# A graph network on one core: some columns of source rows selected by TensorE instead of gathered

## The chip, the cores and the metric

The kernel runs on one core of a Trainium2 chip. The metric is the device time of one execution in microseconds; the figure for the kernel before is the median of 3 runs, 18,531.41 us (18,529.7 to 18,533.06). The core has TensorE (PE, matrix products), VectorE (DVE), ScalarE (ACT), GpSimd (POOL) and SyncE (SP). The first four have instruction queues of their own and meet through semaphores; POOL issues the indirect DMAs (gathers and scatters) and SP the plain ones.

## What is computed

A graph has 12,500 nodes with 32 features and 400,000 edges `src -> dst`, sorted by `dst`. Three attention layers and one edge network run over it:

```
def _gat(x, edge_index, W, att_s, att_d, bias, heads, ch, neg_slope):
    h = (x @ W.T).reshape(n, heads, ch)
    a_s = (h * att_s[None]).sum(-1)
    a_d = (h * att_d[None]).sum(-1)
    src, dst = (edge_index[0], edge_index[1])
    logits = jax.nn.leaky_relu(a_s[src] + a_d[dst], neg_slope)
    m = jax.ops.segment_max(logits, dst, num_segments=n)
    ex = jnp.exp(logits - m[dst])
    denom = jax.ops.segment_sum(ex, dst, num_segments=n)
    alpha = ex / (denom[dst] + 1e-16)
    out = jax.ops.segment_sum(alpha[:, :, None] * h[src], dst, num_segments=n)
    return out.reshape(n, heads * ch) + bias
...
e_feat = jnp.concatenate([x[rol], x[col], edge_attr], axis=-1)
h = jax.nn.relu(e_feat @ W1 + b1)
v = h @ W2 + b2
x_cand = jax.ops.segment_max(v, col, num_segments=num_nodes)
return jnp.maximum(x_cand, x[:, -v.shape[-1]:])
...
x = _layernorm(x + _L0_gnn_ref(x, ...))
x = _layernorm(x + _L1_gnn_ref(x, edge_index, edge_attr_32, ...))
```

Layers 1 and 2 have two heads of 16 channels, with an elu and a clip between the layers; layer 3 has one head of 32. What matters here is `h[src]` and `a_s[src]`, and `x[rol]` in the edge network: for every edge a row of a node table is needed, in an order that only the data know.

## The kernel before

The edges lie on 128 partitions, 3,125 consecutive edges on each; "column t" is edge t of every partition. The work goes through the columns in chunks of T = 60, with four shorter chunks at the end (48, 32, 29 and 16), 54 chunks per stage. There are four stages: `attention(1)`, `attention(2)`, `attention(3)` and `edge_network`; stage 2 and the edge network go through the columns backwards.

For each chunk, `gather` (line 68) issues one indirect DMA per column. It fetches 128 rows, one for each partition, from a table in DRAM (`table1`, or `tables[2]` to `tables[4]`) into a tile `g` (`xs` in the edge network), by the row numbers in `src_i`, `src_last` or `src_first`. So each stage has 3,125 gathers, all in POOL's queue. `gpool` has four `g` buffers and POOL runs ahead of the others by as many chunks as there are free buffers. A row of table 1 holds 36 numbers, those of the later tables 34, 33 and 32.

The rest of a chunk in an attention stage is a chain over DVE, ACT and PE. DVE forms the logits (`lg`, line 697), a running maximum by a scan (line 704), ACT their exponentials (line 715), DVE multiplies the gathered rows with them (`gf`, line 723) and sums them along each run of equal `dst` by scans (line 734). `divided` (lines 494 to 501) divides by the sum and adds the bias. In stages 1 and 2 `finish` then forms the elu on ACT (lines 510 to 512, 521) and goes through the chunk in four blocks of 16 columns (12 in the last): `yb` (line 523), a transpose to `yt` (line 525), two matmuls with the next layer's weights (lines 528 and 529), transposes back to `tb` and `at` (lines 531 and 532). In stage 3 `finish3` adds the node's own row and runs a layer norm on DVE and ACT. Sums go to `sums`, the rows of the next table to `tables[li + 1]`, both by SP's DMAs. In the edge network a chunk has, for each of four blocks, three transposes (lines 870 to 872), twelve half-passes of matmuls (line 877), two activations, two more products (line 883) and a transpose back (line 884), then scans, a maximum, an addition and a layer norm.

Since a node's row is written once per edge of the run, the later tables are indexed by edge: `last_i` and `first_i` hold, for each of the 98 x 128 nodes, the row where its run ends or begins. Between stages a few small transfers join the runs that cross a partition's edge (`s`, `merge_i`), and 98 scatters (`move`, lines 624 to 627) put the input rows where stage 3 reads them. At the start there are 98 gathers of `found` and 98 scatters of `give`; at the end 98 gathers of `so` bring the result into node order.

The order of the instructions on each engine is set when the kernel is built: a scheduler lays out the whole program, by dependences and by its own estimate of when things come due. Each engine then runs its own list in that order.

Of the kernel before, what the change touches and what calls it, by code (L numbers as in the profile page):

```python
# [24 lines left out]
def gnn_resnorm_kernel(ctx: ExitStack, tc: tile.TileContext, a: dict, out: bass.AP):  # L25

# [13 lines left out]
    nc = tc.nc  # L40
# [42 lines left out]

    groups = [(c0, min(28, NC - c0)) for c0 in range(0, NC, 28)]
# [19 lines left out]
    gpool = gstack.enter_context(tc.tile_pool(name="g", bufs=4, side="right"))  # L104
# [4 lines left out]
    x0 = runs.tile([P, NC, D], F32, name="x0")  # L109
# [22 lines left out]
    fixed = ctx.enter_context(tc.tile_pool(name="fixed", bufs=1, space=PSUM)).tile([P, 512], F32, name="fixed")  # L132
    own = const.tile([P, 1], F32, name="own")
    nc.gpsimd.iota(own, pattern=[[1, 1]], base=E + NN, channel_multiplier=1,
                   allow_small_or_imprecise_dtypes=True)
    zeros = const.tile([P, 1250], F32, name="zeros")
# [59 lines left out]

    table1 = dram.tile([NN, D + 4], F32, name="table1")
# [10 lines left out]
    def clear(table, part=0, parts=1):  # L208
        flat = edge_rows(table).rearrange("p t w -> p (t w)")
        k = TE * table.shape[1] // parts  # L210
        z = next(z for z in range(1250, 0, -1) if k % z == 0)
# [86 lines left out]
    cont = runs2.tile([P, TE + 1], F32, name="cont")  # L298
    src_last = runs2.tile([P, TE], I32, name="src_last")
# [14 lines left out]
    with tc.tile_pool(name="seg", bufs=1) as sp, tc.tile_pool(name="rowsp", bufs=2) as rp, \  # L314
# [52 lines left out]
        for c0, n in groups:  # L367
            rows = rp.tile([P, 28, SB], I32, name="found")
            for c in range(n):
                gather(rows[:, c, :], dst_d, find_i[:, c0 + c:c0 + c + 1])  # L370
            less = rp.tile([P, 28, SB], BF16, name="less")[:, :n, :]
            nc.vector.tensor_tensor(less, rows[:, :n, :], bcast(node_p[:, c0:c0 + n, None], [P, n, SB]), op=ALU.is_lt)
            nc.vector.tensor_reduce(r[:, c0:c0 + n], less, axis=AX.X, op=ALU.add)
            nc.vector.tensor_add(first[:, c0:c0 + n], first[:, c0:c0 + n], r[:, c0:c0 + n])
# [15 lines left out]
        nc.sync.dma_start(out=node_rows(table1), in_=tb)  # L390

# [111 lines left out]
    def finish(li, pool, psum, den, v, n, hb=1):  # L503

        y = pool.tile([P, D * T], F32, name="y")[:, :D * n].rearrange("p (f t) -> p f t", t=n)
# [11 lines left out]
        for b in range(0, n, TB):  # L517
# [8 lines left out]
            ph = psum.tile([P, TB * D], F32, name="ph", bufs=hb)[:, :w]  # L526
# [3 lines left out]
            at = pool.tile([P, TB, D], F32, name="at")[:, :nt, :]  # L530
# [19 lines left out]
    def finish3(pool, psum, den, v, x, n):  # L550
# [4 lines left out]
        layernorm(pool, den[:, 2 * T:], x, n)  # L555

    def empties():
# [4 lines left out]
        with tc.tile_pool(name="empty", bufs=2) as ep, tc.tile_pool(name="emptyps", bufs=1, space=PSUM) as eps:  # L562
# [66 lines left out]
    def attention(li, idx):  # L629
# [10 lines left out]
        with tc.tile_pool(name=f"s{li}", bufs=2) as sp, tc.tile_pool(name=f"f{li}", bufs=2) as fp:  # L640
# [18 lines left out]
            with tc.tile_pool(name=f"ps{li}", bufs=1, space=PSUM) as psp, \  # L659
                    tc.tile_pool(name=f"fps{li}", bufs=1, space=PSUM) as fps:  # L660

                small_p = psp.tile([P, 512], F32, name="small_p")
                den = small_p[:, 128:]
                old = None
                for c, (t0, n) in enumerate(todo):
                    g = gpool.tile([P, T * (D + 4)], F32, name="g")[:, :n * w].rearrange("p (t w) -> p t w", w=w)
                    for t in range(n):
                        gather(g[:, t, :], table, idx[:, t0 + t:t0 + t + 1])
# [44 lines left out]
                    rx = psp.tile([P, heads, 512], F32, name="rx", bufs=3 - heads)  # L713
# [5 lines left out]
                    for h in range(heads):  # L719
                        nc.scalar.activation(  # L720
                            rx[:, h, :FS * (n + 1)].rearrange("p (k t) -> p k t", t=n + 1),
                            bcast(rr[:, h:h + 1, :], [P, FS, n + 1]), AF.Exp)
                        nc.vector.tensor_mul(v[:, h * wd:h * wd + ch, cur].rearrange("p f t -> p t f"),  # L723
                                             g[:, :, h * ch:(h + 1) * ch], bcast(wt[:, h, :, None], [P, n, ch]))
                        nc.scalar.copy(v[:, h * wd + ch, cur], wt[:, h, :])  # L725
# [4 lines left out]
                    for h in range(heads):  # L730
                        for f in range(0, wd, FS):
# [226 lines left out]
```

## Time and profile before

| what | value |
|---|---|
| median of 3 runs | 18,531.41 us |
| the profiled execution, its own time | 16,382.21 us |
| its span, first to last instruction | 16,379.3 us |
| gathers of `g` and `xs`, lines 68 | 4 x 3,125 |
| POOL busy | 12,218.7 us (75%) |
| DVE busy | 6,836.7 us (42%) |
| ACT busy | 2,899.1 us (18%) |
| PE busy | 2,781.3 us (17%) |
| mean granted PE clock | 0.578 of full speed |

The four stages show up in a table of busy time by stretch. The columns after the stretch and its length are busy microseconds and instruction counts of PE, its weight loads (PEld), DVE, ACT and POOL, then the granted clock, the share of the DMA engines and GB/s:

```profile
350.00:4250.00 3900.00, 618.47 (x812) 214.74 (x812) 1450.33 (x2532) 799.68 (x1140) 2933.02 (x3099) 0.56 0.27 59
4450.00:8230.00 3780.00, 566.60 (x796) 206.58 (x796) 1387.15 (x2332) 774.32 (x1108) 2859.00 (x3022) 0.57 0.22 44
8450.00:12180.00 3730.00, 0.00 (x0) 0.00 (x0) 1344.37 (x1553) 487.81 (x453) 2820.63 (x2984) 0.50 0.24 54
12310.00:16180.00 3870.00, 1483.15 (x3244) 640.80 (x3244) 2347.93 (x2578) 720.17 (x873) 2910.53 (x3079) 0.68 0.24 65
```

The profile is one execution, and its own time is given beside its span; it differs from the median of the runs by 2,149 us. A line of the groups names line, engine, operation, tiles and count, then busy microseconds and the mean nanoseconds of one, then the idle time just before and what ended most of it. A timeline line has start and duration in microseconds, and in brackets the idle time before and its releaser.

### The profile page before, as it was taken

What the parts mean: (1) busy time and instruction counts of PE and PEld (TensorE: products, weight loads), DVE (VectorE), ACT (ScalarE), POOL (GpSimd) and SP (SyncE); (2) the same over time, 40 slices, a digit from 0 to 9 for tenths busy, and PEclk for the clock granted to TensorE, in tenths of its full rate; (3) what the DMA queues carried; (4) which work ended last, traced back from release to release, by engine and by line L of the source; (5) the groups of instructions that cost most, each with busy time, mean ns of one, the idle gap of its engine ahead of it and who ended that gap; (6) DMA issues with size and microseconds to landing.
All of it is one profiled execution on the core that took longest, in us unless ns stands there. A gap on an engine that the chain in (4) does not pass through costs nothing.

```text
span 16379.3 us, 42394 instructions
## 1 busy us (share of the span) xinstructions
PE 2781.3 (17%) x5140; PEld 1116.2 (7%) x5140; DVE 6836.7 (42%) x9700; ACT 2899.1 (18%) x3835; POOL 12218.7 (75%) x12921
## 2 busy tenths in 40 slices
PE   0111111111111111111100000000003333334342
PEld 0000000000000000000000000000001111111110
DVE  2433333333333333333333333333335666666654
ACT  0221212121212222121211111111111111111111
POOL 6777777777777777777777777777767777777775
PEclk5555555555555555555555555555556666666676
DMA  4222222222222222222222222222222222222221
GB/s 59 71 60 69 60 55 73 55 48 42 43 41 47 41 44 44 43 45 41 46 47 58 51 56 53 56 53 55 54 57 59 66 66 64 66 66 64 69 63 42
DMA packets 580809, 897.63 MB, mean 55 GB/s; under 512 B 286271, under 2 KB 490238, under 8 KB 567070
## 3 DMA queue, kind: packets, MB, share of 16 engines
q0 software_dynamic: 413088, 226.62, 12.5%
q1 hardware_dynamic: 167116, 665.01, 11.5%
q10 hardware_dynamic: 304, 3.20, 0.1%
q14 instruction: 259, 2.11, 0.0%
q8 instruction: 42, 0.69, 0.0%
HBM read 390.67 MB, written 503.27 MB: 55 GB/s over the span
## 4 chain that ended last, share of the span: by engine, by line
POOL 71%; issue 23%; DMA 3%; DVE 1%; PE 0%; ACT 0%; POOLq 0%; DVEq 0%; ACTq 0%
POOL g L68 52%; POOL xs L68 17%; DMA g<-table,src_i 1%; DMA g<-table,src_last 1%; DMA xs<-table,src_last 1%; DMA g<-table,src_first 1%; POOL give L72 1%; POOL so L68 1%; POOL x_e L72 1%; PE ph L877 0%; DMA s<-sums,at_i 0%; PE pv L883 0%; DVE vf L887 0%; DVE z L803 0%; ACT xd L889 0%
## 5 line engine op out<-in xcount | busy, mean ns | idle before, releaser
L68 POOL DMA_INDIRECT g<-table,src_i x3125 | 2958.5, 947 | 989.6 <-issue 940.2
L68 POOL DMA_INDIRECT g<-table,src_last x3125 | 2957.1, 946 | 952.7 <-issue 938.1
L68 POOL DMA_INDIRECT xs<-table,src_last x3125 | 2954.9, 946 | 955.4 <-issue 936.8
L68 POOL DMA_INDIRECT g<-table,src_first x3125 | 2955.7, 946 | 952.7 <-issue 940.8
L697 DVE TENSOR_TENSOR lg<-g,af 128x60 f32<-128x60 f32 (+4 forms) x270 | 59.3, 250 | 4422.3 <-DMA g<-table,src_first 2333.3
L528 PE MATMUL ph<-yt,w_bd 128*128 128x512 f32 (+2 forms) x840 | 669.2, 893 | 3434.1 <-DVE yt L525 3434.1
L529 PE MATMUL pa<-yt,a_bd 128*128 128x512 f32 (+2 forms) x840 | 656.7, 878 | 3307.4 <-DVE at L532 3307.0
L877 PE MATMUL ph<-xt,wb_bd 128*128 128x512 f32 (+2 forms) x832 | 466.1, 645 | 2419.0 <-DVE xt L870 2419.0
L683 DVE CAST src_last<-g 128x60 int32<-128x60 f32 (+4 forms) x54 | 12.7, 235 | 2056.4 <-DMA g<-table,src_i 2056.4
L738 ACT COPY rows<-mx 128x120 f32<-128x120 f32 (+3 forms) x162 | 49.9, 308 | 4419.8 <-DVE mx L704 4366.5
L737 ACT COPY rows<-gf 128x2040 f32<-128x2040 f32 (+3 forms) x162 | 628.4, 3879 | 648.4 <-DVE gf L734 648.4
L734 DVE TENSOR_TENSOR_SCAN gf<-rx,gf 128x488 f32<-128x488 f32 (+4 forms) x918 | 731.9, 858 | 1.4 <-ACT gf L725 0.9
L591 PE MATMUL pt<-ident,tops 128*34 128x128 f32 (+1 forms) x3 | 1.0, 322 | 3954.6 <-DVE xr L548 3952.9
L723 DVE TENSOR_TENSOR gf<-g,small_p 128x960 f32<-128x960 f32 (+5 forms) x270 | 597.8, 2214 | 63.1 <-ACT small_p L715 63.1
L523 DVE SCALAR_TENSOR_TENSOR yb<-y,pe 128x512 f32<-128x512 f32 (+2 forms) x420 | 268.7, 640 | 605.2 <-ACT pe L521 586.7
L533 ACT COPY tb<-at 128x32 f32<-128x32 f32 (+4 forms) x420 | 92.3, 220 | 2333.8 <-DVE at L532 2333.8
L528 PEld LDWEIGHTS ph<-yt,w_bd 128*128 128x128 f32 x840 | 218.6, 287 | 3845.7 <-DVE yt L525 3367.3
L879 ACT ACTIVATE ht<-ph,b_c 128x512 f32<-128x512 f32 (+2 forms) x416 | 275.1, 661 | 1144.0 <-PE ph L877 1140.2
L529 PEld LDWEIGHTS pa<-yt,a_bd 128*128 128x128 f32 x840 | 220.3, 278 | 3681.9 <-DVE at L532 3511.5
L877 PE MATMUL ph<-et,wb_bd 128*128 128x512 f32 (+2 forms) x832 | 450.1, 626 | 0.0
L877 PE MATMUL ph<-xst,wb_bd 128*128 128x512 f32 (+2 forms) x832 | 431.2, 602 | 34.3 <-DVE xst L872 34.3
L883 PE MATMUL pv<-ht,w_bd 128*128 128x512 f32 (+2 forms) x832 | 415.3, 593 | 6.1 <-DVE vf L884 2.0
(295 smaller groups left out, 8591.8 us busy)
## 6 DMA issues: line engine op xcount, KB each, us to landing
sums<-rows SPq DMA_DIRECT2D x100, 1080.0 KB, 4.2
table<-tb SPq DMA_DIRECT2D x50, 1020.0 KB, 4.1
sums<-rows SPq DMA_DIRECT2D x50, 1020.0 KB
g<-table,src_i POOLq DMA_INDIRECT x3125
x_e<-zeros SPq DMA_DIRECT2D x10, 5000.0 KB, 16.8
g<-table,src_last POOLq DMA_INDIRECT x3125
g<-table,src_first POOLq DMA_INDIRECT x3125
xs<-table,src_last POOLq DMA_INDIRECT x3125
```

The lines of the kernel that those rows point to most:

```text
L68: return nc.gpsimd.indirect_dma_start(out=dst, out_offset=None, in_=table, in_offset=bass.IndirectOffsetOnAxis(ap=idx, axis=0))
L72: return nc.gpsimd.indirect_dma_start(out=table, in_=src, in_offset=None, out_offset=bass.IndirectOffsetOnAxis(ap=idx, axis=0))
L523: nc.vector.scalar_tensor_tensor(yb, y[:, :, b:b + nt], 3.0, pe, op0=ALU.min, op1=ALU.add)
L528: nc.tensor.matmul(ph, lhsT=w_bd, rhs=yt, start=True, stop=True)
L529: nc.tensor.matmul(pa, lhsT=a_bd, rhs=yt, start=True, stop=True)
L533: nc.scalar.copy(tb[:, b:b + nt, D:], at[:, :, :heads])
L723: nc.vector.tensor_mul(v[:, h * wd:h * wd + ch, cur].rearrange("p f t -> p t f"), g[:, :, h * ch:(h + 1) * ch], bcast(wt[:, h, :, None], [ ...
L734: nc.vector.tensor_tensor_scan(turned(gf[:, o:o + k], rev), turned(rx[:, h, :k], rev), turned(gf[:, o:o + k], rev), 0.0, op0=ALU.mult, op1 ...
L737: nc.scalar.copy(rows[:, :, :gw], v[:, :, cur].rearrange("p f t -> p t f"))
L877: nc.tensor.matmul(ph, lhsT=wb_bd[:, s, h, :], rhs=x, start=(s == 1), stop=(s == 0))
L879: nc.scalar.activation(ht, ph, AF.Relu, bias=b1_c[:, h:h + 1])
L883: nc.tensor.matmul(pv, lhsT=w2_bd[:, h, :], rhs=hts[h], start=(h == 0), stop=(h == 1))
```

## The change

In stages 1 to 3 one column in 7 and in the edge network one in 12 is no longer gathered row by row. Instead all 12,544 node rows (98 x 128) are held in SBUF, split into three bf16 parts whose sum is the f32 row (`parts`), and TensorE selects the rows. Node number n is written as q, n's partition (n divided by 98), k, one of 7 groups of columns, and b, one of 14 columns in the group. For one column of edges, `fetch` does this:

- two matmuls (L252 of the changed kernel) spread `q + 128 k` of the 128 edges over all partitions (`places_p`);
- DVE compares it with `kid`, giving 7 one-hot matrices 128 x 128 in bf16 (`oh`, L255), and makes a mask for b (`bm`, L258);
- 21 matmuls (7 groups x 3 parts, L262) add up in PSUM (`acc`) the 14 node rows of the right partition and group;
- DVE masks all but the right one (`mine`, L265) and sums over the 14 (L266) into the column of `g`.

In stage 1 the parts come from the node table that is in SBUF anyway; before stages 2, 3 and 4 `node_parts` gathers the node rows with 98 gathers. `Fetch` works out q, k and b for all its columns at the start of a stage. To make room, `g` and `xs` have three buffers instead of four, `rows`, `y`, `at` and `ph` one instead of two, the tile of zeros is half as long, `found` comes in groups of 14, the small PSUM tiles move into `fixed`, `rx` is split by head and its scans follow each head's product, and the edge network's `z` is written over `xs`.

```
+    KT, KN = 7, 14
+    EVERY = {1: 7, 2: 7, 3: 7, 4: 12}
...
-    gpool = gstack.enter_context(tc.tile_pool(name="g", bufs=4, side="right"))
+    xpool = gstack.enter_context(tc.tile_pool(name="x", bufs=1, side="right"))
+    gpool = gstack.enter_context(tc.tile_pool(name="g", bufs=3, side="right"))
...
+    small_p, places_p = fixed[:, 128:384], fixed[:, 384:]
...
+    def split(pool, k, rows, w):
+        rows = rows.rearrange("p b w -> p w b")
+        hi, mid, lo = (parts[:, i, k, :KN * w].rearrange("p (w b) -> p w b", b=KN) for i in range(3))
+        r = pool.tile([P, D + 4, KN], F32, name="rest")[:, :w, :]
+        nc.scalar.copy(hi, rows)
+        nc.vector.tensor_sub(r, rows, hi)
+        nc.scalar.copy(mid, r)
+        nc.vector.tensor_sub(r, r, mid)
+        nc.scalar.copy(lo, r)
...
+        def __contains__(self, t):
+            return bool(self.every) and t < TE // self.every * self.every and t % self.every == self.every - 1
+
+        def fetch(self, psum, g, t, to, bufs=2):
+            if t not in self:
+                return
+            pool, w, i = self.pool, self.w, t // self.every
+            for j in range(2):
+                nc.tensor.matmul(places_p, lhsT=bcast(self.at[:, j, i:i + 1], [P, P]), rhs=ident_b,
+                                 start=(j == 0), stop=(j == 1))
+            oh = pool.tile([P, KT, P], BF16, name="oh")
+            nc.vector.tensor_tensor(oh, bcast(places_p[:, None, :], [P, KT, P]), bcast(kid[:, :, None], [P, KT, P]),
+                                    op=ALU.is_equal)
+            bm = pool.tile([P, KN], F32, name="bm")
+            nc.vector.tensor_scalar(bm, count[:, :KN], self.b[:, i:i + 1], None, op0=ALU.is_equal)
+            acc = psum.tile([P, 512], F32, name="acc", bufs=bufs)[:, :KN * w]
+            for k in range(KT):
+                for part in range(3):
+                    nc.tensor.matmul(acc, lhsT=oh[:, k, :], rhs=parts[:, part, k, :KN * w],
+                                     start=(k == part == 0), stop=(k == KT - 1 and part == 2))
+            mine = pool.tile([P, D + 4, KN], F32, name="mine")[:, :w, :]
+            nc.vector.tensor_mul(mine, acc.rearrange("p (w b) -> p w b", b=KN), bcast(bm[:, None, :], [P, w, KN]))
+            nc.vector.tensor_reduce(g[:, to, :w], mine, axis=AX.X, op=ALU.add)
+
+    def node_parts(li, idx, w):
+        with tc.tile_pool(name=f"np{li}", bufs=2) as pool:
+            for k in range(KT):
+                rows = pool.tile([P, KN, D + 2], F32, name="noderows")[:, :, :w]
+                for b in range(KN):
+                    gather(rows[:, b, :], tables[li], idx[:, k * KN + b:k * KN + b + 1])
+                split(pool, k, rows, w)
...
                     for t in range(n):
-                        gather(g[:, t, :], table, idx[:, t0 + t:t0 + t + 1])
+                        if t0 + t not in fetch:
+                            gather(g[:, t, :], table, idx[:, t0 + t:t0 + t + 1])
+                    for t in range(n):
+                        fetch.fetch(psp, g, t0 + t, t)
...
                 for t in range(n):
-                    gather(xs[:, t, :], tables[4], src_last[:, t0 + t:t0 + t + 1])
+                    if t0 + t not in fetch:
+                        gather(xs[:, t, :], tables[4], src_last[:, t0 + t:t0 + t + 1])
+                for t in range(n):
+                    fetch.fetch(pfp, xs, t0 + t, t, bufs=1)
...
-                z = vp.tile([P, T, D], F32, name="z", bufs=1)[:, :n, :]
+                z = xs[:, :n, :]
```

The scheduler's order on DVE in a chunk of stage 1, from the list of instructions of the changed kernel: after y (L585) come the first oh of the next chunk, then the four blocks of `finish`, with the first `mine` after the first transpose and the second oh in the last block; then for each further column `mine`, the next column's oh, the sum. On PE the 21 matmuls of a column stand directly ahead of the two small ones of the next column. In stage 3 all columns' passes stand behind the layer norm of the chunk before, and in stage 4 too, where the last `mine` follows `xf` and three of its scans.

## Prediction

> **What bounds the kernel now.** I read the page first: shares, then the chain that ended last, then the groups.
>
> ```profile
> PE 2781.3 (17%) x5140; PEld 1116.2 (7%) x5140; DVE 6836.7 (42%) x9700; ACT 2899.1 (18%) x3835; POOL 12218.7 (75%) x12921
> ...
> POOL 71%; issue 23%; DMA 3%; DVE 1%; PE 0%; ACT 0%; POOLq 0%; DVEq 0%; ACTq 0%
> ...
> L68 POOL DMA_INDIRECT g<-table,src_i x3125 | 2958.5, 947 | 989.6 <-issue 940.2
> ```
>
> Four groups of 3125 gathers fill the kernel: 0.947 us each and 0.30 us of issue between two, 1.25 us per gather, 75 us per chunk of 60. POOL and its issue are 94% of the chain. VectorE (DVE) works 42%, but what counts is the length of its own chain in a chunk. The timeline of DVE in stage 1:
>
> ```profile
> 1017.65 0.21 DVE L683 CAST src_last<-g 128x60 int32<-128x60 f32 x1 [39.72 <-DMA g<-table,src_i]
> ...
> 1043.30 2.15 DVE L501 TENSOR_TENSOR y<-y,fixed 128x1920 f32<-128x1920 f32 x1
> 1051.76 0.69 DVE L523 SCALAR_TENSOR_TENSOR yb<-y,pe 128x512 f32<-128x512 f32 x1 [6.30 <-ACT pe L521]
> ```
>
> DVE sat idle 39.7 us until the gathers were in. Its waits in stage 4 (12310 to 16180 us) look different:
>
> ```profile
> DVE xt L870 <- PE ph L877: 347.5, 99, 5.5
> DVE xst L872 <- DMA xs<-table,src_last: 321.6, 68, 17.7
> DVE et L871 <- PE ph L877: 275.1, 103, 5.1
> ```
>
> Columns: us in total, times, longest. Over 52 chunks DVE waits only 6.2 us per chunk for gathers; 75.05 - 6.2 = 68.9 us are its chain with TensorE and ScalarE. In stage 3 one chunk's chain runs from 10022.4 to 10053.0, 30.6 us.
>
> The speed of TensorE (PE) comes from two places of its timeline:
>
> ```profile
> 40.49 2.24 PE L335 MATMUL p_all<-under,is_hi 128*128 128x99 bf16 x25 [4.74 <-DVE under L329]
> ```
>
> ```profile
> 14060.46 2.07 PE L877 MATMUL ph<-xt,wb_bd 128*128 128x512 f32 x2 [45.71 <-DVE xt L870]
> 14062.33 1.92 PE L877 MATMUL ph<-et,wb_bd 128*128 128x512 f32 x2
> 14064.03 1.56 PE L877 MATMUL ph<-xst,wb_bd 128*128 128x512 f32 x2
> 14065.43 1.02 PE L877 MATMUL ph<-xt,wb_bd 128*128 128x512 f32 x2
> 14066.29 1.02 PE L877 MATMUL ph<-et,wb_bd 128*128 128x512 f32 x2
> ```
>
> 25 bf16 pairs of weight load and matmul take 2.24 us, 81 ns apart, so the loads hide. After 45.7 us of idleness a record of 512 columns comes every 0.85 us; 4.5 us later every 0.43.
>
> **What the Trainium skill says.** "TensorE: Matmul & The Clock Gate", Part 1: PE runs at half rate until it has been busy for about 3.4 us; the second fence agrees. The same page, "Back-to-back issue gap": N/1.2 ns cold (99 columns: 82.5, seen 81) and N/2.4 + 2.5 ns warm; no warm bf16 matmul stands in this trace, so 504 columns at 212.5 ns is an estimate from that page. It also gives a sustained 131 ns for N=512, which I keep as the lower bound. The table at its head calls DVE a strict FIFO: an instruction that waits holds up all behind it.
>
> **The change, part by part.** It removes 446 gathers in each of stages 1 to 3 and 260 in stage 4 (1,598) and adds 98 at the start of stages 2, 3 and 4 (294). POOL's chunk falls from 60 gathers to 51.4 (55 in stage 4): 64.3 us (68.8).
>
> Each selected column ("pass") costs two small matmuls (L252), a comparison oh (L255), 21 matmuls into acc (L262), mine (L265) and a sum (L266). The order of DVE's instructions decides: oh of one column, mine of the same, oh of the next, sum, mine of the next. mine waits for the 21 matmuls, the next oh stands behind mine, and PE has nothing before that oh. The two never overlap, although oh and acc have two buffers. One pass in stage 1: oh 1.08 (TENSOR_TENSOR 128x896 in the first 430 us: 1.088), hand-over to PE and weights 0.15, 21 x 0.2125 = 4.46, drain 0.2 (a pair lasts 1.02 against 0.86), mine 0.6 (L523, 512 elements, starts 0.60 apart): 6.5 us. The sum and bm lie beside PE. With 476, 462 and 448 columns: 6.2, 6.05 and 5.95. PE is busy about 70% of a pass with pauses of 2 us; in stage 4 it stays warm across pauses of 2 us, so I count it warm.
>
> Chunk of stage 1 (8.57 passes):
> - from the cast to the end of y: 27.8 us in the trace, less 12.3 of the previous chunk's yb, yt, tb, at and their waits, 15.5; 16.5, as the waits for ACT lose that cover
> - ACT's 6.3 us, which hide the first oh and, cold, its matmuls (4 us at 0.42, the rest at 0.21: 6.4)
> - four blocks of finish with the first mine and second oh: 12.6
> - second burst, 4.8; 6.57 further passes, 42.7; last mine and sum, 1.2
>
> Sum 84.1. Stage 2, with 0.3 less per pass and no casts: 81.6. Stage 3: 30.6, a cold first pass 8.1, 7.57 x 6.05 = 45.8, sum 0.6: 85.1. Stage 4: 68.9, cold first pass 7.9, three at 5.95, the fifth hidden under xf and its scans but for 2.6, less 3.3 for transposes moved into waits and a warmer PE: 94.0. All exceed POOL's 64.3 and 68.8, so DVE's chain sets the pace and POOL waits for g or xs to come free; three buffers instead of four cost nothing then.
>
> Sum over 52.08 chunks of 60 (3125 columns): 344.8 x 52.08 = 17,957. Rest, each from the trace: before the first gathers flow, 387; first chunk of each stage, 64+64+64+69 for its gathers less 176 of passes beneath, 85; four short chunks per stage, 1.9 more fixed shares of 12 us each, 92; three changes of stage, 20 for the merge, 122.5 for 98 gathers, 3 for splitting the last, 437; merge and final 98 gathers, 150. The moves (98 x 1.26 us) now lie beside DVE's tail. Splitting x's table in stage 1 and the divisions (0.5 us each) lie beside found and give, POOL's 196 transfers. Single buffers for y, at, rows and ph cost nothing at these distances (a chunk apart; ph is freed by the transpose ahead of its reuse); uncovered, under 1 us each per chunk. The small matmuls share one PSUM bank with biases and sums (places_p, small_p): nothing where the next column's run behind the burst, as PE's order has them, 0.3 us per pass if a wait on that bank keeps them until after mine; I take nothing. The burst itself lies between 21 x 0.131 = 2.75 us and, cold, 21 x 0.42 = 8.8 us; I take 4.46. Smaller zero rows: nothing, x_e is needed two stages later. Total 19,110 against the profiled execution's 16,382.
>
> **Against the median.** The runs take 18,531.4, 2,149 more than the profiled execution (16,382.2), and no view shows where. I take it to lie with POOL, nearly the whole chain: over 12,900 transfers 0.167 us each, a gather at 1.417. DVE's chain would then be as in the profile, and only what waits for POOL outright grows: found and give (196), 294 node gathers, four first chunks (209), the final 98: 797 x 0.167 = 133. Forecast 19,110 + 133 = 19,240 us, 3.8% slower. The other end, everything stretched by 1.131, is a rival.
>
> **Rivals.**
> 1. The 13% hits every engine: 19,110 x 1.131 = 21,620; as a fixed amount, 21,260. For: the same work in the same state. Against: a factor on DVE and PE has no sign in the trace. Chance 0.22.
> 2. PE stays cold between passes: 4.4, 4.1, 4.0 and 3.9 us more per pass, 52.08 x (7.57 x 12.5 + 4 x 3.9) = 5,740, so 24,980. For: the mean granted clock is 0.5 to 0.6 now. Against: the warm stretch above. 0.06.
> 3. The other side: matmuls sustain the page's 131 ns, the burst is 2.75 us and a pass 4.8. Chunks fall to 71, 69.5, 73.5 and 88; against POOL's 72.9 (at 1.417) the stages take 72.9, 72.9, 73.5 and 88 x 52.08 = 16,010, in all 17,290, faster by 6.7%. It decides from 0.5 us per pass (719 us over 1,391 exposed passes), a matmul under some 188 ns; a shorter DVE chain than mine would do the same. Against: a record of 512 columns now takes exactly two cycles per column at the full clock. 0.09.
>
> A same result needs my chain 3.8% too long: 0.02. The forecast keeps 0.61.
>
> **Numbers.** Time 19,240. Its own range, 4% on the chains, is 18,500 to 20,000; to leave out no more than 2 in 10 the range must reach rival 1, so 18,500 to 21,700. Within 0.2% (about what a measurement can tell from no change): 0.02. Faster: 0.09 of rival 3 and 0.02 of the forecast's tail, 0.11. Slower 0.87.
>
> **What would show it.** Right: DVE and PE fill the chain, POOL idles on g and xs, acc bursts start about 6.5 us apart with a clock near 0.9, stages take 4.4, 4.25, 4.4 and 4.9 ms in the profile. Wrong: bursts of 21 matmuls well under 4.4 us or near 9; oh starting before the mine ahead of it; POOL still 94% of the chain; a difference between profile and runs that stays at 13%.

## The result: 28,578 us, and the profile after

The changed kernel takes 28,578.24 us (median of 4 runs, 28,570.02 to 28,584.67) against 18,530.72 of the kernel before: a ratio of 1.542, 95% interval 1.5395 to 1.5448. Forecast were 19,240 us and at most 21,700: the sign was right, the size missed by 9,340 us. Here the profiled execution and the runs agree (28,579.82 us; span 28,577.0).

One thing has to be known ahead of all else: the runs of this study are of two kinds. The eighteen later ones fell on nine chips, each used at one time only. On six of them the kernel before takes 16,347 to 16,378 us (kind A below), on three 18,531 to 18,556 (kind B). By their times, the profile of before that the prediction read (16,382) is of kind A, and the runs that decide, before and after, are of kind B. Whether the kind belongs to the chip or to a condition at that time isn't known.

The page of the changed kernel, kind B: the busy times, the chain, and the groups that answer to those shown of before.

```profile
PE 11030.1 (39%) x41894; PEld 4801.0 (17%) x41894; DVE 10720.2 (38%) x16242; ACT 2961.8 (10%) x3919; POOL 11020.6 (39%) x11618
...
PE 29%; another core or an unknown queue 29%; DVE 29%; issue 7%; ACT 3%; POOL 2%; DMA 0%; DVEq 0%; ACTq 0%; SPq 0%; POOLq 0%
...
L265 DVE TENSOR_TENSOR mine<-acc,bm 128x504 f32<-128x504 f32 (+3 forms) x1598 | 1041.1, 652 | 12868.3 <-remote 7477.3
...
L71 POOL DMA_INDIRECT g<-table,src_i x2679 | 2535.7, 947 | 3994.4 <-DVE gf L817 3156.0
```

POOL no longer bounds: it is busy 39% and waits for g to come free. VectorE (DVE) and TensorE (PE) do fill the chain, but they get only 58% of it; for another 29% the profile names no engine of the core. The third line says where it is: 7,477 of the 12,868 us that DVE waits ahead of mine end with "remote": the semaphore's update is on record, but no instruction that makes it had ended in the 1.5 us before. In the program mine waits for PE alone. Its timeline in one chunk of stage 2 (start, duration; in brackets the idle time before and what ended it):

```profile
9055.94 6.19 PE L262 MATMUL acc<-parts,oh 128*128 128x476 bf16 x21
...
9063.53 0.58 DVE L616 STREAM_TRANSPOSE at<-pa 128x384 f32<-128x384 f32 x1 [4.39 <-PE fixed L252]
...
9085.60 0.94 POOL L71 DMA_INDIRECT g<-table,src_last  x1 [0.30 <-issue]
...
9093.63 0.66 DVE L265 TENSOR_TENSOR mine<-acc,bm 128x476 f32<-128x476 f32 x1 [29.39 <-remote]
...
9102.32 0.65 DVE L265 TENSOR_TENSOR mine<-acc,bm 128x476 f32<-128x476 f32 x1 [6.35 <-PE acc L262]
...
9108.46 0.65 DVE L265 TENSOR_TENSOR mine<-acc,bm 128x476 f32<-128x476 f32 x1 [3.79 <-PE acc L262]
...
9114.60 0.65 DVE L265 TENSOR_TENSOR mine<-acc,bm 128x476 f32<-128x476 f32 x1 [3.79 <-PE acc L262]
```

The 21 matmuls are recorded as done at 9062.13, yet mine starts at 9093.6, 7 us after the last gather of POOL's run ended (9086.5). The trace also holds the updates of PE's semaphore. Those of the 21 matmuls and of the two small ones behind them, which end at 9062.25, stand at 9093.60 and 9093.65. So they came over 31 us after the recorded ends and closer together than the ends are, as if both had been held up after they were made. With POOL silent an update stands 0.02 us after the end (9102.30 for 9102.28). This goes by POOL's runs throughout the profile. In runs of 60 to 70 us, of 272 recorded waits of DVE and ScalarE (ACT) for a PE instruction that ended 35 to 65 us into the run, 236 were released more than 1.5 us after that end; where it ended 75 us or more after the run's start, none of 1,739 was.

From 9102.3 on a pass takes 6.14 us, as forecast (6.2). In a later run of the same kernel on kind B, mine's longest pause ends a median of 7.3 us after POOL's run in stages 1 and 2 (7.15 to 7.95 for the middle 8 in 10 of 49 chunks each). The Trainium skill warns of reading a matmul's end too literally ("Perfetto Trace Analysis", section "Tensor Engine Instruction (MATMUL, LD_WEIGHTS)"): the end in the profile is estimated, and the semaphore goes out only once PSUM has acknowledged the writes. 31 us are far beyond that, and the ends that the estimate gives are right once POOL is silent.

So POOL's gathers and the passes, which the prediction laid side by side, run nearly one after the other.

### The profile page after: what moved, and what is told of

It reads as the page before. It is cut to its first block, busy times and chain, and to the rows that moved or that the text cites. A ratio compares the mean times of both kernels' runs of the same rounds, so it can differ in the third digit from the quotient of the medians.

```text
span 28577.0 us, 122498 instructions
## 1 busy us (share of the span) xinstructions
PE 11030.1 (39%) x41894; PEld 4801.0 (17%) x41894; DVE 10720.2 (38%) x16242; ACT 2961.8 (10%) x3919; POOL 11020.6 (39%) x11618
## 4 chain that ended last, share of the span: by engine, by line
PE 29%; another core or an unknown queue 29%; DVE 29%; issue 7%; ACT 3%; POOL 2%; DMA 0%; DVEq 0%; ACTq 0%; SPq 0%; POOLq 0%
PE acc L262 21%; DVE oh L255 5%; PE ph L973 4%; DVE mine L265 3%; DVE gf L823 3%; DVE gf L817 2%; PE pv L979 1%; DVE y L581 1%; DVE y L585 1%; PE ph L612 1%; PE pa L613 1%; POOL noderows L71 1%; DVE vf L983 1%; DVE fixed L624 1%
## 5 line engine op out<-in xcount | busy, mean ns | idle before, releaser
L262 PE MATMUL acc<-parts,oh 128*128 128x504 bf16 (+3 forms) x33558 | 8294.7, 410 | 10470.3 <-DVE oh L255 7532.9
L262 PEld LDWEIGHTS <-oh 128*128 128x128 bf16 x33558 | 3505.5, 108 | 14893.6 <-DVE oh L255 7796.0
L265 DVE TENSOR_TENSOR mine<-acc,bm 128x504 f32<-128x504 f32 (+3 forms) x1598 | 1041.1, 652 | 12868.3 <-remote 7477.3
L71 POOL DMA_INDIRECT g<-table,src_i x2679 | 2535.7, 947 | 3994.4 <-DVE gf L817 3156.0
L71 POOL DMA_INDIRECT g<-table,src_last x2679 | 2539.9, 948 | 3833.0 <-DVE gf L817 3031.1
L71 POOL DMA_INDIRECT g<-table,src_first x2679 | 2540.7, 948 | 3690.1 <-DVE ad L780 2723.3
L252 PE MATMUL fixed<-ident_b,fat 128*128 128x128 bf16 x3196 | 464.9, 230 | 5426.6 <-DVE y L585 1943.5
L255 DVE TENSOR_TENSOR oh<-fixed,kid 128x896 bf16<-128x896 f32 x1598 | 1728.2, 1081 | 647.7 <-remote 444.6
L252 PEld LDWEIGHTS <-fat 128*128 128x128 bf16 x3196 | 303.4, 99 | 5814.2 <-issue 3347.6
L266 DVE TENSOR_REDUCE g<-mine 128x36 f32<-128x504 f32 (+2 forms) x1338 | 859.0, 642 | 5.6
L817 DVE TENSOR_TENSOR gf<-g,fixed 128x960 f32<-128x960 f32 (+5 forms) x270 | 602.2, 2230 | 76.8 <-ACT fixed L804 72.5
```

Source lines behind the costliest of these rows:

```text
L71: return nc.gpsimd.indirect_dma_start(out=dst, out_offset=None, in_=table, in_offset=bass.IndirectOffsetOnAxis(ap=idx, axis=0))
L252: nc.tensor.matmul(places_p, lhsT=bcast(self.at[:, j, i:i + 1], [P, P]), rhs=ident_b, start=(j == 0), stop=(j == 1))
L255: nc.vector.tensor_tensor(oh, bcast(places_p[:, None, :], [P, KT, P]), bcast(kid[:, :, None], [P, KT, P]), op=ALU.is_equal)
L262: nc.tensor.matmul(acc, lhsT=oh[:, k, :], rhs=parts[:, part, k, :KN * w], start=(k == part == 0), stop=(k == KT - 1 and part == 2))
L265: nc.vector.tensor_mul(mine, acc.rearrange("p (w b) -> p w b", b=KN), bcast(bm[:, None, :], [P, w, KN]))
L266: nc.vector.tensor_reduce(g[:, to, :w], mine, axis=AX.X, op=ALU.add)
```

## Experiments

Time per chunk is read from the starts of ScalarE's copies into rows (stages 1 to 3) and xd (stage 4): 40 chunks, or 17 to 20 full ones where a half stage is meant. The two kernels in numbers, us per chunk of 60 columns:

| | stage 1 | 2 | 3 | 4 |
|---|---|---|---|---|
| before, kind A | 75.0 | 75.0 | 75.0 | 75.0 |
| forecast for after | 84.1 | 81.6 | 85.1 | 94.0 |
| after, kind A | 84.9 | 82.4 | 85.8 | 99.0 |
| after, kind B | 126.4 | 124.0 | 120.9 | 155.3 |

### Is it TensorE's instructions, the gathers, or GpSimd's running? (kind A)

The kernel before again; the changed kernel without gathers; with a third of the matmuls; with twice as many half as wide.

> The kernel before, unchanged, to learn where its 18,531 us go that the profiled execution of 16,382 us doesn't show. If the gathers themselves are slower in the timed executions (the prediction's assumption), this one's profile, if it is near 18,531, shows 1.41 us from gather to gather in place of 1.25, with the recorded 947 ns or the issue part grown. If it is something around the gathers (VectorE or TensorE late), the gathers keep 1.25 us and POOL has waits it did not have.

> The changed kernel with the 51 to 55 gathers of every chunk left out: one plain transfer of a chunk's bytes from the front of the table stands for them (the rows are then not those of src). TensorE's and VectorE's work is the same. Theory A (gathers in flight hold up what TensorE hands to VectorE): mine's 26 us of waiting per chunk go, the passes keep 6.4 / 6.1 / 6.0 / 5.9 us, chunks take 84 / 82 / 85 / 94 us as predicted and the kernel 18,800 to 19,600. Theory B (TensorE's own many instructions pile up somewhere, with or without gathers): the waits stay, near 28,000. Theory C (VectorE shut out by GpSimd from the memory they share): as A here. Theory D (TensorE runs out of fetched instructions): the waits stay, near 28,000.

> The changed kernel with the first of the three bf16 parts alone: 7 matmuls per pass in place of 21 (the selected rows are then rounded to bf16). The pass loses 14 x 0.209 = 2.9 us. Theory A or B or D with a cost per TensorE instruction: 18 in place of 46 per pass, so the 26 us per chunk fall to some 10 or, if only what is over some stock counts, to nothing: 16,000 to 19,500. Theory C (a wait that goes by POOL's run and VectorE alone): 26 us per chunk stay: 28,577 - 1,598 x 2.9 = 23,900.

> The changed kernel with each of the 21 matmuls of a pass split into two of half the columns: 88 TensorE instructions per pass in place of 46 for the same columns. Per-instruction theories (A with a cost per instruction, B, D): the wait of mine doubles or more, 7,477 us to 15,000, with pass time at most a few us longer: 36,000 to 42,000. Theory C: the wait stays; only what the shorter matmuls add to a pass is seen (about 1 us x 1,598): 28,600 to 30,500.

```
-  gather(g[:, t, :], table, idx[:, t0 + t:t0 + t + 1])     # per column      (e2)
+  nc.gpsimd.dma_start(out=g, in_=first rows of table)      # one per chunk
-  for part in range(3):                                                      (e3)
+  for part in range(1):
-  nc.tensor.matmul(acc, ...parts[:, part, k, :KN * w])                       (e4)
+  nc.tensor.matmul(acc[:, half], ...parts[:, part, k, half])   # for two halves
```

Measured: 16,378, 19,370, 15,767 and 19,488 us, beside 16,372 of the kernel before. e4, with all of the change's gathers and twice its matmuls, had no late mine at all: chunks of 85.8 / 82.6 / 85.8 / 99.0. e1, the kernel before, has 1.25 us per gather, so it doesn't explain 18,531. All expectations had taken it for granted that the waits would be there to be removed; on this chip they were not, and the four runs left the question open. e2 says one thing: 84.9 / 82.4 / 85.8 / 99.0 with the gathers and without them, so on kind A they are fully hidden.

### The program or the chip?

The changed kernel as it is, and with the next column's oh made ahead of the current mine:

```
   oh = select(first column)
   for each column:
+      ahead = select(next column)      # L252 and oh, ahead of mine
       21 matmuls into acc; mine; sum
+      oh = ahead
```

> The changed kernel, unchanged. In the last four runs the kernel before took 16,372 us, not 18,531, and twice the TensorE instructions ran without the 26 us waits. Theory E (the waits and the 18,531 belong to a condition of the chip or of its recording in the runs of the result, not to the program): where the kernel before takes 16,372 beside it, this takes 19,110 to 19,500 with passes of 6.4 / 6.1 / 6.0 / 5.9 us and mine released by TensorE; where the kernel before takes 18,531 beside it, 28,578 with the waits. Theory F (the waits belong to this very stream of instructions, which the split and the thinned kernels changed): 28,578 whatever the kernel before takes.

> The changed kernel with the next column's places and oh made ahead of the current column's mine, so that TensorE's 21 matmuls of two columns follow on each other. If a pass is a serial chain of oh, matmuls and mine (the prediction), it shortens from 6.2 to TensorE's own 4.4 + 0.45 = 4.9 us in stages 1 to 3 and some 5.5 in stage 4 (one acc buffer): 1,338 x 1.3 + 260 x 0.4 = 1,850 us less than the changed kernel beside it: about 17,400 where that takes 19,200. If the 26 us waits are there, POOL's 64 us and the passes still don't overlap: over 25,000.

> As the last, but only one column in 10 in stages 1 to 3 and none in stage 4 (nor its 98 gathers). Chunks of stages 1 and 2: VectorE and TensorE 37 + 6 x 4.9 = 66, POOL 54 x 1.25 = 67.5 us; stage 3 31 + 29 = 60 against 67.5; stage 4 75 as before. Three stages save 6 x 1.25 x 52 = 390 us each, and 196 gathers and their parts cost some 400: 15,600 where the kernel before takes 16,372, faster than both. With the 26 us waits in it: over 20,000.

> The changed kernel, unchanged, once more: in the last three runs the kernel before took 18,531 us beside it, in the four before them 16,372. Theory E (the 26 us waits of mine come with the condition in which the kernel before takes 18,531): if the kernel before takes 16,372 beside this run, 19,110 to 19,500, mine released by TensorE, nearly all of the gathers' 200,000 semaphore updates in the trace. Theory F (they belong to this stream of instructions): 28,578 in either.

> The changed kernel with the next column's places and oh made ahead of the current mine. Where the kernel before takes 16,372: a pass of 4.9 us (5.5 in stage 4) in place of 6.2, 1,850 us less than the changed kernel: 17,200 to 17,600. Where it takes 18,531: 26,367 as measured.

> The same with one column in 10 in stages 1 to 3 and none in stage 4. Where the kernel before takes 16,372: POOL bounds it again, three stages save 390 us each and 196 gathers and their parts cost some 400: 15,500 to 15,800, 3 to 5% faster than before. Where it takes 18,531: 23,730 as measured.

| us (ratio to before) | kind B (e5 to e7) | kind A (e8 to e10) |
|---|---|---|
| before | 18,531 | 16,347 |
| after | 28,579 (1.542, 1.5394 to 1.5445) | 19,425 (one run) |
| oh ahead | 26,367 (1.423, 1.4206 to 1.4253) | 16,621 (one run) |
| oh ahead, one in 10, none in stage 4 | 23,730 (1.280, 1.2777 to 1.282) | 15,453 (0.9454, 0.9438 to 0.947) |

Theory E (the waits come with the kind) holds, F (they come with the program) falls: the same program has the waits on one kind and not on the other. Of e8 (kind A) the page's busy times and chain, then the wait of mine (us in total, times, longest), then the timeline in stage 2:

```profile
PE 10052.9 (52%) x41894; PEld 4544.4 (23%) x41894; DVE 10686.6 (55%) x16242; ACT 2962.2 (15%) x3919; POOL 10976.4 (57%) x11618
...
PE 45%; DVE 40%; POOL 6%; issue 4%; ACT 4%; DMA 1%; DVEq 0%; ACTq 0%; POOLq 0%
```

```profile
DVE mine L265 <- PE acc L262: 5638.8, 1510, 7.0
```

```profile
7023.77 4.39 PE L262 MATMUL acc<-parts,oh 128*128 128x476 bf16 x21 [1.63 <-DVE oh L255]
7023.99 0.94 POOL L71 DMA_INDIRECT g<-table,src_last  x1 [0.30 <-issue]
...
7028.20 0.65 DVE L265 TENSOR_TENSOR mine<-acc,bm 128x476 f32<-128x476 f32 x1 [3.79 <-PE acc L262]
...
7034.34 0.65 DVE L265 TENSOR_TENSOR mine<-acc,bm 128x476 f32<-128x476 f32 x1 [3.79 <-PE acc L262]
```

The 29% without a named engine are gone, every wait of mine but a few is ended by PE, and the longest is 7 us. With gathers 1.25 us apart around it, mine starts 0.04 us after the burst, 6.14 us after the one before. Making oh ahead of mine gains 2,804 us on kind A, more than the 1,850 expected: stage 1's chunk falls by 15.6 us, 1.8 per pass, so a pass costs 4.6. e10 makes POOL the bound again (67.1 / 67.5 / 67.4 / 74.9 us, as expected) and beats the kernel before on kind A by 5.5%; on kind B it is 28% slower. POOL's longest waits in e10:

```profile
POOL g L71 <- issue: 2526.7, 8291, 0.3
POOL xs L71 <- issue: 950.5, 3119, 0.3
```

They are the 0.3 us between two gathers, and nothing else of size.

e7's stage 4 has no selected columns and yet takes 123.2 us a chunk on kind B, 74.9 on kind A (e10). Two of its waits, for ph, in e7 (18000 to 22000 us) and in e10 (12000 to 15000):

```profile
DVE et L970 <- remote: 800.5, 67, 26.9
```

```profile
DVE et L970 <- PE ph L976: 208.7, 80, 3.1
```

So the late hand-offs aren't special to acc and mine.

### What makes the hand-offs late? (kind B)

One kernel with four experiments, one with eight half stages, and the kernel before:

> Four experiments in one kernel, one to a stage of the changed kernel; read from each stage's time per chunk. Stage 1: the 51 gathers of a chunk left out, one plain transfer for them. Stage 2: the first of three bf16 parts alone, 7 matmuls per pass. Stage 3: each of the 21 matmuls split in two halves of the columns, 42 with the same columns in all. Stage 4: the 55 gathers left out, POOL writes zeros for some 1.2 us in place of each, then one plain transfer. (The rows are then not those of src; stage 2's are rounded.) On a chip like the one of the last call the chunks take 84.9 / 64.3 / 85.8 / 99.0 us whatever the theory. On a chip where the kernel before takes 18,531 (the changed kernel: 126.5 / 124.2 / 120.9 / 155.3): Theory G (the semaphore updates of the gathers, 16 each, crowd out TensorE's hand-offs): stage 1 84.9 and stage 4 99; stage 3 about 121 if the cost is per hand-off, 140 to 160 if per TensorE instruction; stage 2 124 - 25 = 99 per hand-off, 75 to 85 per instruction. Theory H (TensorE's own many instructions, with or without gathers): stages 1 and 4 stay at 126 and 155, stage 2 falls to 75 to 85, stage 3 grows to 140 to 160. Theory C (GpSimd's running, not its transfers): stage 1 84.9, stage 4 155.

> The kernel before, unchanged, for its stages: where it takes 16,350 to 16,380 they are 75.0 us per chunk each. On a chip where it takes 18,531 it is 2,150 us longer. The prediction put that to POOL's gathers, evenly: 75.0 to 84.9 in each stage, 1.417 us from gather to gather. Theory G puts it where TensorE works while POOL gathers: gathers 1.25 us, stage 4 near 75 + 2,150 / 52 = 116, stages 1 to 3 near 75.

> Eight halves of stages in one kernel, read from the time per chunk of each half. Stage 1: first half without gathers (one plain transfer a chunk), second half as the kernel before (60 gathers, no selected columns). Stage 2: as changed, then with 7 matmuls per pass. Stage 3: as changed, then each matmul split in two. Stage 4: POOL writes zeros for 1.2 us in place of each gather, then as the kernel before (60 gathers, no selected columns). (Rows are not those of src where gathers are left out, and rounded with 7 matmuls.) Where the kernel before takes 16,350 to 16,380: 84.9, 75.0; 82.4, 64.3; 85.8, 85.8; 99, 75. Where it takes 18,531: theory G (updates of the gathers against TensorE's hand-offs): 84.9, 75 to 80; 124, then 99 if per hand-off and 75 to 85 if per instruction; 121, then 121 per hand-off and 140 to 160 per instruction; 99, then 116 to 123. Theory H (TensorE's many instructions alone): 126, 75; 124, 80; 121, 150; 155, 75. Theory C (GpSimd's running): 84.9, 75; 124, 99; 121, 121; 155, 123. The prediction's own reading (every gather is 13% slower there): 84.9, 85; 82, 73; 86, 86; 99, 85.

> The last kernel again, for a chip on which the kernel before takes 18,531 us. There theory G (semaphore updates of the gathers against TensorE's hand-offs): stage 1 84.9, 75 to 80; stage 2 124, then 99 if per hand-off and 75 to 85 if per TensorE instruction; stage 3 121, then 121 per hand-off and 140 to 160 per instruction; stage 4 99, then 116 to 123. Theory H (TensorE's many instructions alone): 126, 75; 124, 80; 121, 150; 155, 75. Theory C (GpSimd's running): 84.9, 75; 124, 99; 121, 121; 155, 123. The prediction's own reading (every gather 13% slower): 84.9, 85; 82, 73; 86, 86; 99, 85. Where the kernel before takes 16,350 to 16,380: 85, 75; 82, 64; 86, 86; 99, 75 again.

e11, e12 and e13 fell on kind A and gave what was expected there (e12: 74.9 in each stage). e14 fell on kind B. us per chunk, of the same kernel on both:

| half stage | e13, A | e14, B |
|---|---|---|
| 1: passes, no gathers | 85.1 | 85.1 |
| 1: gathers, no passes (as before) | 73.7 | 80.9 |
| 2: as changed | 82.6 | 124.6 |
| 2: 7 matmuls in place of 21 | 58.9 | 101.8 |
| 3: as changed | 85.7 | 121.6 |
| 3: 42 half matmuls | 85.6 | 127.4 |
| 4: passes, POOL writes zeros | 99.0 | 99.0 |
| 4: gathers, no passes | 71.4 | 123.5 |

(A second half bound by POOL comes out a little short, as POOL has run ahead by the switch: e11 has 64.3 for the 58.9, e12 74.9 for the 71.4.) e14's waits of mine in stage 1 without gathers (1500 to 2500 us), and in stage 2 with 7 matmuls (8700 to 10500):

```profile
DVE mine L272 <- PE acc L269: 358.7, 97, 4.0
```

```profile
DVE mine L272 <- remote: 251.8, 18, 18.9
...
DVE mine L272 <- PE acc L269: 158.8, 104, 3.1
```

Without gathers, kind B runs at kind A's speed to the tenth of a microsecond, with POOL idle (85.1) or busy otherwise (99.0): theories C (POOL's running) and H (TensorE's many instructions) fall. A third of the matmuls saves 22.8 us, about the matmuls' own time (8.57 x 14 x 0.201 = 24.1), and twice the instructions add 5.8: the lateness hardly depends on how many instructions PE has. What is late is what PE hands on while gathers run.

### Rate, updates or rows?

> The changed kernel with its gathers changed in stages 2 and 3. Stage 2: a plain transfer fills g, then each gather fetches 64 of the 128 rows (first half of the stage) or 16 (second half; the other rows are not those of src). Stage 3: POOL writes zeros 3 times (first half) or once (second half) for some 0.35 us after each gather, so gathers come some 2.3 and 1.6 us apart in place of 1.25. Where the kernel before takes 18,531: if the waits follow the semaphore updates (16 a gather whatever its rows), stage 2 stays near 124 in both halves; if they follow rows or descriptors, it falls to 85 to 100 in the second. If the waits need a rate of gathers above some limit, stage 3's first half has no waits of mine beyond TensorE's own (chunk 117 to 120, POOL's time), the second some; if any gather under way holds TensorE's hand-offs up, mine waits until POOL's end, and chunks take POOL's 117 and 82 us and 45 to 60 more. Where it takes 16,350: stage 2 82 to 90, stage 3 117 to 120 and 86.

> The kernel before, unchanged, for its stages where it takes 18,531. Theory G (TensorE's hand-offs are late while POOL gathers, as in the last run's halves without selected columns): gathers 1.25 us apart in stages 2 and 3, stage 4 near 116 to 121 us per chunk in place of 75, most of the 2,150 us. The prediction's assumption: every gather 1.42 us apart, 85 us per chunk in all four stages.

> Stages 1 and 4 as in the kernel before (60 gathers a chunk, no selected columns). Stage 2 as changed, with g filled by one plain transfer and each gather fetching 64 of the 128 rows (first half of the stage) or 16 (second half). Stage 3 as changed, with POOL writing zeros 3 times (first half) or once (second half) for 0.42 us right after each gather: gathers some 2.5 and 1.7 us apart in place of 1.25. (In the last run but one these writes had been moved ahead of stage 3, so that it said nothing of the pace.) Where the kernel before takes 16,350: 75 in stages 1 and 4, 82 to 86 in stage 2, 128 and 86 in stage 3. Where it takes 18,531: stage 1 75 to 82, stage 4 116 to 121, gathers 1.25 us apart (the prediction's assumption: 85 in both, 1.42 us). Stage 2 stays near 124 if the waits follow the 16 updates of a gather, and falls to 85 to 100 in its second half if they follow its rows. Stage 3: if the waits need a rate of gathers above a limit between 2.5 and 1.25 us, its first half has none and takes 128, POOL's own time; if any gather under way holds TensorE's hand-offs up, 128 + 45 to 60 and 85 + 45 to 60.

> The last kernel again, for a chip on which the kernel before takes 18,531: stage 1 75 to 82, stage 4 116 to 121, gathers 1.25 us apart (the prediction's assumption: 85 in both, 1.42 us). Stage 2 near 124 in both halves if the waits follow the 16 updates of a gather, 85 to 100 in the second if they follow its rows. Stage 3: no waits of mine beyond TensorE's own and 128 us in the first half if they need a rate of gathers above a limit between 2.5 and 1.25 us; 128 + 45 to 60 and 85 + 45 to 60 if any gather under way holds TensorE's hand-offs up. Where it takes 16,350, the times of the last run again.

```
   gather(g[:h, t, :], table, idx[:h, ...])    # stage 2: h = 64, then 16 rows
+  for _ in range(3):  nc.gpsimd.memset(zeros[:, :384], 0.0)    # stage 3; second half: range(1)
```

e15 to e17 fell on kind A; in e15 the zeros had also been moved out of stage 3, so it says nothing of the pace. e18 is e17 on kind B:

| half stage | e17, A | e18, B |
|---|---|---|
| 1: as before, 60 gathers | 74.1, 75.0 | 79.7, 84.0 |
| 2: gathers of 64, of 16 rows | 82.6, 82.5 | 130.1, 130.0 |
| 3: gathers 2.49 us apart | 128.8 | 128.7 |
| 3: gathers 1.55 us apart | 85.6 | 85.6 |
| 4: as before, 60 gathers | 74.9 | 123.2, 123.3 |

DVE's waits in e18, stage 2 with 64 rows (6000 to 8000 us):

```profile
DVE mine L269 <- remote: 492.4, 15, 45.4
DVE mine L269 <- PE acc L266: 417.3, 107, 6.6
```

and stage 3 with one write of zeros after each gather (15200 to 17200 us):

```profile
DVE mine L269 <- PE acc L266: 647.8, 164, 6.9
DVE mine L269 <- issue: 97.9, 29, 3.7
```

("issue" is a wait that nothing in the trace explains; here it is at most 3.7 us, what a pass's matmuls take.) Of DVE's recorded waits for PE in e18, none of 140 is released over 1.5 us late with gathers 1.55 us apart and none of 192 with 2.49; in stage 2, where fewer rows bring the gathers to 1.21 and 1.15 us, 74 of 264 and 100 of 260 are. It is their rate. An eighth of the rows changes little, so what counts is one gather, not its bytes. The Trainium skill ("DMA: Bandwidth & Descriptors", section "Why a DMA increments its semaphore by 16 and not by 1") says what stays the same: a transfer of POOL posts 16 semaphore updates whatever its shape. On kind A the trace agrees: e17 holds 15.9 to 16.3 of them per gather in every half stage, with 128, 64 and 16 rows.

The groups of stage 1, 60 gathers a chunk and no passes; first e17, then e18:

```profile
L71 POOL DMA_INDIRECT g<-table,src_i x3125 | 2955.8, 946 | 994.8 <-issue 937.7
```

```profile
L71 POOL DMA_INDIRECT g<-table,src_i x3125 | 3315.1, 1061 | 1068.5 <-issue 1025.9
```

Kept up, gathers come 1.40 us apart on kind B in the mean (83 to 85 us a chunk); half of them within 1.30, and one in ten over 1.5. 16 updates in 1.40 us are 11.4 per us; POOL at 1.25 us posts 12.8, at 1.55 us 10.3. An estimate from these: a run of gathers closer than 1.40 us leaves a backlog that lasts beyond its end by what each gather is short of 1.40. Beside it, the median time from the last gather of a run to the first late update of PE:

| gathers of a run | us apart | backlog, estimated | first late update |
|---|---|---|---|
| 51, result's profile, stages 1 to 3 | 1.25 | 7.6 | 7.1 |
| 55, result's profile, stage 4 | 1.25 | 8.2 | 8.7 |
| 51 of 64 rows, e18 | 1.21 | 9.7 | 9.6 |
| 51 of 16 rows, e18 | 1.15 | 12.6 | 12.3 |

The rate taken from stage 1 gives the ends of the waits in the others within 0.5 us. The number of updates on record fits: of e8's by transfers the trace holds 200,098, of the same kernel's in e5 52,414; and e18 holds 14.8 to 15.9 per gather in stage 3, whose gathers are 1.55 us or more apart, 1.4 to 3.4 in the other stages. That the lost records and the late updates have one cause isn't shown.

## Why the prediction missed

- *POOL falls from the bound, DVE's chain with PE takes over, POOL waits for g and xs:* right, on both kinds.
- *The order oh, matmuls, mine, next oh, without overlap; 6.5 / 6.2 / 6.05 / 5.95 us a pass:* right: 6.41, 6.14, 6.00 and 5.87 (stage 4 of e8). e6 and e9 show it from the other side.
- *21 matmuls of 504 columns warm, 4.46 us, and 0.2 of drain:* right: 4.64 in e8's stage 1, start to start 0.213 us against the 0.2125 estimated from the Trainium skill ("TensorE: Matmul & The Clock Gate", section "Back-to-back issue gap"), and 0.376 for the last; 4.39, 4.27 and 4.15 us in the later stages. Rival 3 (0.131, a faster kernel) and rival 2 (cold throughout) are out.
- *Chunks of 84.1 / 81.6 / 85.1 / 94.0 and 19,110 us in the frame of the profiled execution:* on kind A 84.9 / 82.4 / 85.8 / 99.0 and 19,425. Stage 4's term was 5.0 us short, 260 of the 315 us. Its passes were priced right: in e8's chunk from 16229.6 to 16328.5 they add 28.1 us to DVE's chain (forecast 28.35). But the 3.3 us credited to transposes and a warmer PE did not come, and the rest of the chain takes 70.8 us, not 68.9.
- *"I take it to lie with POOL ... a gather at 1.417":* close, where it could be measured: stage 1 as before takes 1.39 (e14) and 1.40 us (e18) a gather. Over 12,500 gathers 0.15 us would be 1,900 of the 2,184 us between the kinds. The kernel before itself was not traced on kind B, so its stages 2 to 4 are not shown.
- *"DVE's chain would then be as in the profile, and only what waits for POOL outright grows: ... 797 x 0.167 = 133":* this step failed. On kind B the gathers are not only slower where they are kept up; while they run, what PE hands to DVE also comes late, and DVE's chain with PE was the new bound. It cost 41.5, 41.6, 35.1 and 56.3 us per chunk (kind B less kind A), 174.5 x 52.08 = 9,088 us in place of 133. That is all but 65 us of what lies between 19,425 and 28,578. Run as before, stage 1 hides what there is of it: in e18 PE's updates come at most 2.7 us late there, and DVE still waits for the gathers (2500 to 4500 us):

```profile
DVE src_last L783 <- DMA g<-table,src_i: 767.8, 24, 33.4
```

- *Rival 1, everything 13% longer:* no. DVE's and PE's own work is no longer on kind B (85.1 and 85.1; 99.0 and 99.0). The late updates are nearly all PE's: in the result's profile 594 of DVE's 2,651 recorded waits for PE are released over 1.5 us late, 3 of ACT's 1,938 for DVE and none of DVE's 554 for ACT. In e18's stage 1, where gathers are kept up, DVE's updates come late too (73 of ACT's 352 waits, up to 4.5 us).
- *Three buffers in place of four cost nothing:* right on kind A, where e17's stages 1 and 4, as before but with three, take 75.0 and 74.9 us. On kind B not settled. e18's stage 4, as before but with three xs buffers, one ph buffer and z written into xs, takes 123 us a chunk there. In the kernel before it can't: 48 x 52 = 2,500 alone exceeds its 2,184. So up to 48 of the 56.3 us that the changed kernel loses in stage 4 may need these changes and no selected column; they were not tried by themselves.

What stays open: what it is that passes 11.4 updates per us, and why there are two kinds. The backlog says when PE's updates come, not why they wait to its end: served in order, one made 39 us into a run would, by the same estimate, be 4.6 us late, not 31. All runs were recorded by the profiler, and none of them was without it; if the recording itself holds the updates up on one kind and not on the other, it would look like this too. One thing speaks against so simple a reading: the result's profile keeps 89% of PE's updates, 84% of DVE's and only 73% of ACT's, yet PE's are the late ones. Passes with gathers held at 1.55 us in all four stages were not tried either. By the half stage (85.6 on both kinds, against 120.9 as changed on kind B) I estimate that this would bring the changed kernel on kind B near its 19,425, still slower than before. No version tried beats the kernel before on both kinds.

## What to carry to other kernels

When the runs and the profiled execution differ by 13%, as here, the profile may be of another condition: find out which engine's work is longer there before any number of it is carried over, and give what is unexplained a path to the new bound, not to the old one alone. Work moved from a bounding engine onto two that hand results to each other is exposed to anything that delays a hand-off; count hand-offs on the new path, not only busy time. Where a profile names no owner for a wait, compare the time of the semaphore's update with the end of the instruction that makes it. A serial pass of three instructions on two engines is worth pipelining before it is worth counting: making oh one column ahead was worth 2,804 us on kind A.

## What was not expected of the hardware

- On three of nine chips gathers that keep coming take 1.40 us each in the mean in place of 1.25, and after some ten microseconds of gathers 1.25 us apart TensorE's semaphore updates come late, up to 57 us. Those still held when a run of 51 gathers ends come 7.1 us after its last one, 12.3 us where the gathers are 1.15 us apart.
- Spaced 1.55 us apart, gathers have no such effect; with 16 or 64 rows in place of 128 they still have it.
- It hardly depends on TensorE's instruction count: with 7, 21 or 42 matmuls per hand-off a chunk differs by at most 6 us beyond the matmuls' own time.
